# Reordering the prologue of a two-layer graph kernel: first loads, first pairs' nodes and propagators, and the preparation of the output weights

## The chip, the cores and the metric

The kernel runs on one core of a Trainium2 chip. The metric is the device time of one execution in microseconds (us): the median of three runs, beside which one further execution was profiled. In the text PE is the matrix engine, DVE the vector engine, ACT the scalar engine, POOL the GpSimd engine and SP the engine that only issues transfers (DMAs). SPq and ACTq are the DMA-issuing instructions of SP and ACT.

## The reference

There are 128 graphs of 128 nodes with 512 features. Layer 0 is an attention over eight heads, layer 1 a hypergraph convolution with a hidden width of 1024; each is followed by a residual sum and a layer norm.

```python
def _L0_gnn_ref(X, A, W, b, a_self, a_neigh):
    feats = jnp.einsum('bnf,hfu->bhnu', X, W)
    e_self = jnp.einsum('bhnu,hu->bhn', feats, a_self)
    e_neigh = jnp.einsum('bhnu,hu->bhn', feats, a_neigh)
    dense = e_self[..., :, None] + e_neigh[..., None, :]
    dense = jax.nn.leaky_relu(dense, negative_slope=0.2)
    dense = dense + NEG_BIG * (1.0 - A[:, None, :, :])
    att = jax.nn.softmax(dense, axis=-1)
    out = jnp.einsum('bhij,bhju->bhiu', att, feats) + b[None, :, None, :]
    ...
    return jax.nn.relu(out)
...
def hypergraph_conv(x, adj, W, b):
    H = (adj != 0).astype(x.dtype)
    w = adj.reshape(N, -1)[:, :C]
    xw = jnp.einsum('ncd,hd->nch', x, W)
    Dn = jnp.einsum('nce,ne->nc', H, w)
    Dn = jnp.where(Dn > 0, 1.0 / Dn, 0.0)
    Be = H.sum(axis=1)
    Be = jnp.where(Be > 0, 1.0 / Be, 0.0)
    m = Be[:, :, None] * jnp.einsum('nce,nch->neh', H, xw)
    out = Dn[:, :, None] * jnp.einsum('nce,neh->nch', H, m)
    return out + b
...
h = jax.nn.relu(hypergraph_conv(x, adj, W1, b1))
h = layer_norm(h, gamma, beta)
return hypergraph_conv(h, adj, W2, b2) + x
...
x = _layernorm(x + _L0_gnn_ref(x, adj, ...))
x = _layernorm(x + _L1_gnn_ref(x, adj, ...))
```

## The kernel before, in words

Graphs are worked two at a time: 64 pairs, p = 0 to 63. Each pair passes five stages of T = 38.6 units of a hand-written clock ("lag" 0 to 4), so that five pairs are in work at once. Every step of a pair is a small Python function with a due time; lines 912 to 933 put all steps of all pairs in one list, sort it by due time and emit it. Due times set nothing but the order: each engine executes its own instructions in that order, waiting for semaphores, and each DMA queue likewise. For the first two pairs, and for work that is done once, the table `first` (lines 893 to 902) and the list `todo` (lines 877 to 891) give own due times. What is emitted in this way before the first full pair is called the prologue here.

The three large weight products use a scheme with seven products of quarter blocks in place of eight, so that each weight matrix needs sums of its blocks. These sums are made once in the prologue: `prepare_first_sums` (L206, by way of `second_sums`, L188) for the attention weights, `prepare_hidden` (L209, its instruction is L215) for the hidden weights, `prepare_output_block_sums` (L255, L192) for the output weights. The output weights are also scaled by gamma and centred first: `prepare_output` (L220) multiplies them by gamma and beta on PE (the tiles pv, 32 matmuls of L228), `prepare_output_sums` (L233) brings these sums to DRAM and back on all partitions (gw, bw_bc), and `prepare_output_blocks` (L245, L250) applies them.

Steps that matter below, for pair p:

- `load` (L95): the adjacency `a` (two buffers) and its first rows `w` (one buffer), by SP. `load_blocks` (L104) loads node features `xb`, `load_edges` (L113) adjacency columns `ab`, one buffer each.
- `nodes` (L303): DVE makes the node degrees from `a` and `w` and transposes them into the tile `dr` (L318), which has one buffer. `write_nodes` (L321, L323) writes `dr` to DRAM (dd_d), `spread_nodes` (L503, L506) reads it back on all partitions into `dnb`, which also has one buffer.
- `edges`, `scale_edges` (L346, L361): the propagator's two factors hT and hB on DVE. `propagator` (L369, L373, PE) multiplies them into pd, `r_evict` (L379, L381, DVE) multiplies pd by `dnb` into R.
- `spread_rows` (L467 on): DVE transposes the attention terms (L473) and SP writes them to DRAM as rd (L481 for pair 0, L483 else). `neighbours` (L491 on, L500) reads them back on all partitions as nb, 2 x 512 KB. Then POOL masks nb (`masked`, L519), ACT applies the leaky relu (L526), DVE takes the maximum (`largest`, L532) and ACT the exponential (L540).
- `attend` (L599, PE, pav), `attended` (L613, L614, DVE), `add_bias` (L623, POOL), `residual` (L630, DVE), `rstds` (L644 DVE, L646 POOL), `first_shift` (L661, DVE), `first_output` (L667, ACT) end layer 0. `propagate` (L690, PE, pz) and the chain ph (L725, PE) start layer 1, `squares` (L776) and `h_sums` (L399) on POOL follow, then the chain py (L417, PE).

SP issues its DMAs in order and stops at one that has to wait. A DMA whose destination buffer is still to be read waits for the last reader, even when that reader comes later in the sorted list on another engine: the load of `ab` for pair 2 has the due time 105.7 and its reader-to-be-awaited `edges` of pair 1 has 110.4.

In the part ahead of the sorted list, SP loads the four blocks of the attention weights (w_raw, L136), then `a` and `w` of pair 0; ACT issues the attention vectors, the node features and edges of pair 0 and the six small vectors (as_bc, an_bc, xb, ab, b0_bc, b2_bc, b1_sb, gb).

Of the kernel before, what the change touches and what calls it, by code (L numbers as in the profile page):

```python
# [8 lines left out]
F32 = mybir.dt.float32  # L9
AF = mybir.ActivationFunctionType  # L10
ALU = mybir.AluOpType
# [9 lines left out]
def kernel(  # L21
# [45 lines left out]
    nc = tc.nc  # L67
    G, N, F = x.shape
    P = 128
    DH = w1t.shape[1]  # L70
# [5 lines left out]
    QU = HALF // 2  # L76
# [3 lines left out]
    B = 32  # L80
    NB = P // B

    const = ctx.enter_context(tc.tile_pool(name="const", bufs=1))
# [11 lines left out]
    def load(p):  # L95
        s = st[p]
        gs = slice(2 * p, 2 * p + 2)
        s["a"] = work.tile([P, 2, N], F32, tag="a", name=f"a_{p}", bufs=2)
        nc.sync.dma_start(s["a"], adj[gs].rearrange("g n e -> n g e"))
        s["w"] = work.tile([P, 2, N], F32, tag="w", name=f"w_{p}")  # L100
        for g in range(2):
            nc.sync.dma_start(s["w"][:, g, :], adj[2 * p + g, 0, :].partition_broadcast(P))

    def load_blocks(p, queue=None):  # L104
        s = st[p]
        gs = slice(2 * p, 2 * p + 2)

        s["xb"] = work.tile([P, 2 * NB, P], F32, tag="xb", name=f"xb_{p}")
        rows = x[gs].rearrange("g (b n) (f c) -> f n (g b) c", b=NB, f=NB)
        for f in range(NB):  # L110
            (queue or nc.sync).dma_start(s["xb"][f * B:(f + 1) * B], rows[f])

    def load_edges(p, queue=None):  # L113
        s = st[p]

        s["ab"] = work.tile([P, 2 * NB, B], F32, tag="ab", name=f"ab_{p}")
        rows = adj[2 * p:2 * p + 2].rearrange("g (b n) (f e) -> f n (g b) e", b=NB, f=NB)
        for f in range(NB):
            (queue or nc.sync).dma_start(s["ab"][f * B:(f + 1) * B], rows[f])


    def block(dst, ap, i, j, rows, cols):
# [8 lines left out]
    w0_sb = const.tile([P, 7, KF // 2, HH, UW], F32, name="w0_sb")  # L131
    w0_12 = work.tile([P, KF // 2, HH, UW], F32, tag="y2", name="w0_12")
# [6 lines left out]
        )  # L139
        w0_blocks.append((dst, raw.rearrange("p k (h u) -> p k h u", h=HH), j))  # L140

    def everywhere(ap, n, name):
        t = const.tile([P, n], F32, name=name)
        nc.scalar.dma_start(t, ap.partition_broadcast(P))
        return t

    as_bc = everywhere(a_self, F, "as_bc")
    an_bc = everywhere(a_neigh, F, "an_bc")
    load(0)
    load_blocks(0, nc.scalar)  # L150
    load_edges(0, nc.scalar)
    b0_bc = everywhere(b0, F, "b0_bc")
    b2_bc = everywhere(b2, F, "b2_bc")
    bw_bc = const.tile([P, F], F32, name="bw_bc")

    b1_sb = const.tile([P, KH], F32, name="b1_sb")
    gb = const.tile([P, 2, KH], F32, name="gb")
    for t, ap in ((b1_sb, b1), (gb[:, 0, :], gamma), (gb[:, 1, :], beta)):
        nc.scalar.dma_start(t, ap.rearrange("(k p) -> p k", p=P))


    w2_sb = const.tile([P, 7, KH // 2, QU + 1], F32, name="w2_sb")
    w2_12 = work.tile([P, KH // 2, QU], F32, tag="hS", name="w2_12")
    w2_blocks = ((w2_sb[:, 0, :, :QU], 0, 0), (w2_12, 0, 1), (w2_sb[:, 1, :, :QU], 1, 0),
                 (w2_sb[:, 2, :, :QU], 1, 1))
# [15 lines left out]
    for i in range(2):  # L181
        t = const.tile([P, 2, H, UW + 1], F32, name=f"ft{i}")
# [2 lines left out]
    dn = const.tile([P, B], F32, name="dn")  # L185
    nc.gpsimd.memset(dn, 0.0)

    def second_sums(w, b12, some=slice(0, 4)):  # L188

        b11, b21, b22, t4, t1, t2, t3 = (w[i] for i in range(7))  # L190
        for dst, in0, in1 in ((t1, b12, b11), (t2, b22, t1), (t3, b22, b12), (t4, b21, t2))[some]:
            nc.vector.tensor_tensor(dst, in0, in1, op=ALU.subtract)  # L192

    def prepare_first(half):
        for n, (dst, raw, j) in list(enumerate(w0_blocks))[2 * half:2 * half + 2]:
# [8 lines left out]
                nc.vector.tensor_reduce(dst[:, :, :, c], t, AX.X, ALU.add)  # L204

    def prepare_first_sums():  # L206
        second_sums([w0_sb[:, i] for i in range(7)], w0_12)

    def prepare_hidden(i):  # L209
        a11, a12, a22, s1, s2, s3, s4 = (w1_sb[:, i] for i in range(7))  # L210
# [41 lines left out]
                    op0=ALU.mult, op1=ALU.subtract,  # L252
                )

    def prepare_output_block_sums(some):  # L255
        second_sums([w2_sb[:, i, :, :QU] for i in range(7)], w2_12, some)

    def prepare_mean_columns():
        for i in (0, 1, 5):
# [610 lines left out]
    def o_norm(p, s):  # L870
# [5 lines left out]
    T = 38.6  # L876
    todo = [
        (11.1, prepare_first, (0,)), (12.0, prepare_first, (1,)), (77.9, prepare_first_sums, ()),
        (11.8, load_blocks, (1,)), (15.65, load, (1,)), (15.7, load_edges, (1,)),
        (15.8, load_weights, (w2_blocks, w2t, DH // 2, QU)),  # L880
        (16.0, load_weights, (w1_blocks[:2], w1t, F // 2, HALF)),
        (80.2, load_weights, (w1_blocks[2:], w1t, F // 2, HALF)),
        (103.0, prepare_output, ()), (116.5, prepare_output_sums, ()),
        (112.0, prepare_hidden, (0,)), (112.5, prepare_hidden, (1,)),
        (114.5, prepare_hidden, (2,)), (115.0, prepare_hidden, (3,)),
        (122.4, prepare_output_blocks, (slice(0, 2),)),
        (128.4, prepare_output_blocks, (slice(2, 4),)),
        (130.6, prepare_output_block_sums, (slice(0, 2),)),
        (132.8, prepare_output_block_sums, (slice(2, 4),)),
        (100.0, prepare_mean_columns, ()),  # L890
    ]

    first = {
        ("nodes", 0): 15.0, ("write_nodes", 0): 16.5, ("spread_nodes", 0): 18.5,
        ("x_transpose", 0): 11.5, ("edges", 0): 15.2, ("scale_edges", 0): 15.4,
        ("spread_rows", 0): 13.5, ("neighbours", 0): 14.0, ("load_rows", 0): 14.2,
        ("propagator", 0): 103.5, ("r_evict", 0): 104.0,
        ("nodes", 1): 17.6, ("write_nodes", 1): 17.9, ("x_transpose", 1): 14.5,
        ("edges", 1): 110.4, ("scale_edges", 1): 110.5,
        ("spread_rows", 1): 79.9, ("neighbours", 1): 80.0,  # L900
        ("propagator", 1): 117.7, ("r_evict", 1): 118.0,
    }
# [9 lines left out]
    for p in range(PAIRS):  # L912
        if p > 1:
            todo.append((p * T, load, (p,)))
            todo.append((p * T + 19.0, load_blocks, (p,)))
            todo.append((p * T + 28.5, load_edges, (p,)))
        for lag, time, name, since, fn, args in steps:
            if p < since:
                continue
            if p == 0 and lag == 2 and time < 8.5:  # L920
                time *= 0.2
            if p == PAIRS - 1:

                time = {
                    ("attend", 0): 24.25, ("attended", 0): 25.5, ("add_bias", 0): 25.6,
                    ("h_sums", 0): 19.1, ("h_sums", 1): 19.2,
                    ("product", 2): 25.0 if (lag, time) > (3, 20.0) else time,
                }.get((name,) + args[:1], time)
            todo.append((first.get((name, p), (p + lag) * T + time), run, (fn, p, args)))
# [46 lines left out]
```

## Time and profile before

| | |
|---|---|
| median of three runs | 2586.89 us (2586.15 to 2587.33) |
| profiled execution | 2588.48 us; span of the trace 2586.4 us |
| busy: PE, DVE, POOL, ACT | 2515.8, 2146.5, 1714.1, 1514.4 us |
| mean granted PE clock | 0.989 |
| first matmul of L454 (attention features of pair 0) | 19.41 us |
| first matmul of pv (L228) | 65.08 us |
| first matmul of pair 1's second-stage pav (L599) | 117.71 us |

Times within the trace count from the first instruction. "Idle before" and "waits" are time in which an engine stood still, with what ended it. A line such as `DMA dd_d<-dr` names a transfer by destination and source. In a timeline each row is a run of equal instructions: start, duration, engine, line, operation, out<-in, number.

### The profile page before, as it was taken

What the parts mean: (1) busy time and instruction counts of PE and PEld (TensorE: products, weight loads), DVE (VectorE), ACT (ScalarE), POOL (GpSimd) and SP (SyncE); (2) the same over time, 40 slices, a digit from 0 to 9 for tenths busy, and PEclk for the clock granted to TensorE, in tenths of its full rate; (3) what the DMA queues carried; (4) which work ended last, traced back from release to release, by engine and by line L of the source; (5) the groups of instructions that cost most, each with busy time, mean ns of one, the idle gap of its engine ahead of it and who ended that gap; (6) DMA issues with size and microseconds to landing.
All of it is one profiled execution on the core that took longest, in us unless ns stands there. A gap on an engine that the chain in (4) does not pass through costs nothing.

```text
span 2586.4 us, 48239 instructions
## 1 busy us (share of the span) xinstructions
PE 2515.8 (97%) x16312; PEld 2274.8 (88%) x16312; DVE 2146.5 (83%) x4650; ACT 1514.4 (59%) x4293; POOL 1714.1 (66%) x1797
## 2 busy tenths in 40 slices
PE   4799999999999999999999999999999999999997
PEld 3699899899999999989899999999989998999996
DVE  4788888888888888888888888888888888888875
ACT  2365565565565565565565665665665665665662
POOL 1567667667667667667667667667667667667753
PEclk8899999999999999999999999999999999999999
DMA  5444444444444444444444444444444444444430
GB/s 146 116 135 132 143 136 132 143 137 132 142 138 132 142 138 132 145 135 132 135 139 137 137 139 136 136 142 134 135 141 137 134 143 135 134 141 137 135 118 33
DMA packets 428250, 345.57 MB, mean 134 GB/s; under 512 B 146658, under 2 KB 377058, under 8 KB 428004
## 3 DMA queue, kind: packets, MB, share of 16 engines
q1 hardware_dynamic: 422132, 340.77, 44.5%
q10 hardware_dynamic: 5872, 1.72, 0.4%
q8 instruction: 130, 2.13, 0.3%
q14 instruction: 116, 0.95, 0.1%
HBM read 240.66 MB, written 101.72 MB: 132 GB/s over the span
## 4 chain that ended last, share of the span: by engine, by line
PE 89%; DMA 4%; DVE 3%; issue 2%; POOL 2%; SPq 0%; ACT 0%; ACTq 0%; POOLq 0%; DVEq 0%
PE phX L725 17%; PE pyX L417 14%; PE phW L725 9%; PE pfX L417 8%; PE pyW L417 8%; PE pav L599 8%; PE phY L725 4%; PE pz L690 4%; PE pq L849 4%; PE pfW L417 4%; PE pyY L417 4%; PE pfY L417 2%; DMA nb<-rd 1%; PE pd L373 1%; DMA dnb<-dd_d 1%
## 5 line engine op out<-in xcount | busy, mean ns | idle before, releaser
L519 POOL TENSOR_TENSOR nb<-nb,neg 128x512 f32<-128x512 f32 x256 | 320.0, 1272 | 117.9 <-DMA nb<-rd 75.0
L725 PEld LDWEIGHTS phX<-zS,w_sb 128*128 128x128 f32 x3072 | 364.8, 193 | 37.5 <-issue 37.5
L293 ACT COPY py<-pyX 128x257 f32<-128x257 f32 (+1 forms) x192 | 71.7, 374 | 548.0 <-PE pyX L417 548.0
L725 PE MATMUL phX<-zS,w_sb 128*128 128x128 f32 x3072 | 376.0, 276 | 7.1 <-issue 7.1
L776 POOL TENSOR_TENSOR sq<-sq 128x512 f32<-128x512 f32 (+2 forms) x384 | 344.9, 898 | 32.4 <-ACT sq L765 11.3
L526 ACT ACTIVATE nb<-nb,ft 128x128 f32<-128x128 f32 x1024 | 325.2, 389 | 50.1 <-POOL nb L519 48.0
L540 ACT ACTIVATE nb<-nb,nm 128x128 f32<-128x128 f32 x1024 | 320.2, 392 | 17.9 <-DVE nm L532 17.9
L646 POOL TENSOR_TENSOR rso<-veo,mhalf 128x2 f32<-128x2 f32 x64 | 44.8, 700 | 344.3 <-DVE veo L644 302.6
L630 DVE SCALAR_TENSOR_TENSOR y<-y,x 128x512 f32<-128x512 f32 x128 | 155.6, 1216 | 137.9 <-POOL y L623 137.9
L599 PEld LDWEIGHTS pav<-ft,eT 128*128 128x128 f32 x2048 | 251.4, 194 | 11.8 <-issue 2.6
L755 ACT ACTIVATE h<-h,b_sb 128x128 f32<-128x128 f32 x768 | 242.1, 392 | 16.9 <-DVE h L740 16.9
L417 PE MATMUL pyX<-w_sb,hS 128*128 128x257 f32 (+1 forms) x1024 | 248.1, 384 | 2.2 <-DVE hS L399 1.8
L599 PE MATMUL pav<-ft,eT 128*128 128x65 f32 x2048 | 246.5, 274 | 2.5 <-DVE eT L561 1.9
L417 PE MATMUL pyW<-w_sb,hS 128*128 128x256 f32 x1024 | 244.1, 380 | 3.7 <-DVE y L808 3.2
L417 PE MATMUL pyX<-w_sb,h 128*128 128x257 f32 (+1 forms) x1024 | 243.2, 379 | 0.0
L623 POOL TENSOR_TENSOR y<-y,b_bc 128x512 f32<-128x512 f32 x128 | 162.1, 1266 | 95.1 <-DVE y L614 95.1
L417 PEld LDWEIGHTS pyW<-w_sb,hS 128*128 128x128 f32 x1024 | 192.1, 189 | 37.2 <-DVE y L808 10.2
L417 PEld LDWEIGHTS pyX<-w_sb,hS 128*128 128x128 f32 x1024 | 190.2, 191 | 28.0 <-issue 2.1
L417 PEld LDWEIGHTS pyX<-w_sb,h 128*128 128x128 f32 x1024 | 189.3, 190 | 24.9
L399 POOL TENSOR_TENSOR xS<-xT 128x256 f32<-128x256 f32 x124 | 117.9, 951 | 89.5 <-DVE xT L337 89.5
L532 DVE TENSOR_REDUCE nm<-nb 128x4 f32<-128x512 f32 x256 | 173.6, 679 | 0.4 <-ACT nb L526 0.4
L293 ACT COPY ph<-phX 128x512 f32<-128x512 f32 x192 | 112.3, 585 | 97.0 <-PE phX L725 93.8
(127 smaller groups left out, 5843.2 us busy)
## 6 DMA issues: line engine op xcount, KB each, us to landing
nb<-rd SPq DMA_DIRECT2D x128, 512.0 KB, 5.9
ed<-nb SPq DMA_DIRECT2D x126, 512.0 KB, 3.2
eb<-ed SPq DMA_DIRECT2D x504, 128.0 KB, 2.9
x<-in_x_dram SPq DMA_DIRECT2D x64, 512.0 KB, 6.9
out_dram<-o SPq DMA_DIRECT2D x64, 512.0 KB, 2.8
xb<-in_x_dram SPq DMA_DIRECT2D x252, 128.0 KB, 3.0
a<-in_adj_dram SPq DMA_DIRECT2D x64, 128.0 KB, 6.1
w<-in_adj_dram SPq DMA_DIRECT2D x128, 64.0 KB, 3.9
```

The costliest lines, as they stand in the source:

```text
L293: nc.scalar.copy(t[:, :n], s[kind, "X"][:, :n])
L417: nc.tensor.matmul(to[:, :n], lhs[:, k, :], rhs[:, k, :n], start=bool(start) and k == 0, stop=(k == nk - 1), skip_group_check=True,)
L519: nc.gpsimd.tensor_tensor(t, t, neg[:, :, None, :].to_broadcast([P, NB, HH, B]), op=ALU.add)
L526: nc.scalar.activation(t, t, AF.Prelu, bias=s["ft"][:, g, h, 0:1], alpha=SLOPE)
L532: nc.vector.tensor_reduce(s["nm"][:, g, hs], scores(p, s, g, hs).rearrange("p b h j -> p h b j"), AX.XY, ALU.max, negate=True,)
L540: nc.scalar.activation(t, t, AF.Exp, bias=s["nm"][:, g, h:h + 1])
L599: nc.tensor.matmul(t[:, h * (U + 1):(h + 1) * (U + 1)], s["eT"][:, g, q * HH + h, :], s["ft"][:, g, q * HH + h, 2:], start=True, stop=True,)
L623: nc.gpsimd.tensor_tensor(s["y"][:, g, :], s["y"][:, g, :], b0_bc, op=ALU.add)
L630: nc.vector.scalar_tensor_tensor(y, y, 0.0, s["x"][:, g, :], op0=ALU.max, op1=ALU.add)
L725: nc.tensor.matmul(to[:, m * N:(m + 1) * N], w[:, k, m * P:(m + 1) * P], rhs[:, k, :], start=bool(start) and m == 0 and k == 0, stop=(k == ...
L755: nc.scalar.activation(dst[:, k, :], src[:, k, :], AF.Relu, bias=b1_sb[:, c:c + 1])
L776: nc.gpsimd.tensor_tensor(t[:, :n, :], t[:, :n, :], t[:, n:2 * n, :], op=ALU.add)
```

## The change

The due times are those of the sorted list. What changes:

- ACT issues two DMAs only (as_bc, an_bc). The node features, `a` and `w`, and the edges of pair 0 are all issued by SP, in this order, after w_raw. The other vectors become a step `load_vectors`, issued by SP at 15.75: gamma, beta, b1 (L159 before), then b0 and b2 on all partitions.
- `write_nodes` of pair 0 goes from 16.5 to 15.72, which is before the output weights (15.8) and half of the hidden weights (16.0); `spread_nodes` of pair 0 from 18.5 to 15.9, between these two.
- `nodes` of pair 1 goes from 17.6 to 79.95, `write_nodes` of pair 1 from 17.9 to 80.1. The first is now after `spread_rows` of pair 1 (79.9) on DVE, and after `load` of pair 2 (77.2) in the list; the second is after `neighbours` of pair 1 (80.0) and before the second half of the hidden weights (80.2) on SP.
- `propagator` of pair 0 goes from 103.5 to 102.9, ahead of `prepare_output`; `r_evict` of pair 0 from 104.0 to 110.3.
- `prepare_hidden` goes from 112.0 to 115.0 to 110.6 to 111.6, `edges` and `scale_edges` of pair 1 from 110.4 and 110.5 to 112.0 and 112.1, `prepare_output_sums` from 116.5 to 114.2.
- `prepare_output_blocks` goes from 122.4 and 128.4 to 123.2 and 125.2. The first two of the four block sums of the output weights move from DVE to POOL and from 130.6 to 125.6, the other two stay on DVE (132.8 to 133.0).

```diff
+    everywhere(as_bc, a_self, nc.scalar)
+    everywhere(an_bc, a_neigh, nc.scalar)
+    load_blocks(0)
+    load(0)
+    load_edges(0)
+
+    def load_vectors():
+        for t, ap in ((gb[:, 0, :], gamma), (gb[:, 1, :], beta), (b1_sb, b1)):
+            nc.sync.dma_start(t, ap.rearrange("(k p) -> p k", p=P))
+        everywhere(b0_bc, b0, nc.sync)
+        everywhere(b2_bc, b2, nc.sync)
...
-    def second_sums(w, b12, some=slice(0, 4)):
+    def second_sums(engine, w, b12, some=slice(0, 4)):
...
-            nc.vector.tensor_tensor(dst, in0, in1, op=ALU.subtract)
+            engine.tensor_tensor(dst, in0, in1, op=ALU.subtract)
...
-        (15.8, load_weights, (w2_blocks, w2t, DH // 2, QU)),
+        (15.75, load_vectors, ()), (15.8, load_weights, (w2_blocks, w2t, DH // 2, QU)),
...
-        (103.0, prepare_output, ()), (116.5, prepare_output_sums, ()),
-        (112.0, prepare_hidden, (0,)), (112.5, prepare_hidden, (1,)),
-        (114.5, prepare_hidden, (2,)), (115.0, prepare_hidden, (3,)),
-        (122.4, prepare_output_blocks, (slice(0, 2),)),
-        (128.4, prepare_output_blocks, (slice(2, 4),)),
-        (130.6, prepare_output_block_sums, (slice(0, 2),)),
-        (132.8, prepare_output_block_sums, (slice(2, 4),)),
+        (103.0, prepare_output, ()), (114.2, prepare_output_sums, ()),
+        (110.6, prepare_hidden, (0,)), (110.7, prepare_hidden, (1,)),
+        (111.5, prepare_hidden, (2,)), (111.6, prepare_hidden, (3,)),
+        (123.2, prepare_output_blocks, (slice(0, 2),)),
+        (125.2, prepare_output_blocks, (slice(2, 4),)),
+        (125.6, prepare_output_block_sums, (nc.gpsimd, slice(0, 2))),
+        (133.0, prepare_output_block_sums, (nc.vector, slice(2, 4))),
...
-        ("nodes", 0): 15.0, ("write_nodes", 0): 16.5, ("spread_nodes", 0): 18.5,
+        ("nodes", 0): 15.0, ("write_nodes", 0): 15.72, ("spread_nodes", 0): 15.9,
...
-        ("propagator", 0): 103.5, ("r_evict", 0): 104.0,
-        ("nodes", 1): 17.6, ("write_nodes", 1): 17.9, ("x_transpose", 1): 14.5,
-        ("edges", 1): 110.4, ("scale_edges", 1): 110.5,
+        ("propagator", 0): 102.9, ("r_evict", 0): 110.3,
+        ("nodes", 1): 79.95, ("write_nodes", 1): 80.1, ("x_transpose", 1): 14.5,
+        ("edges", 1): 112.0, ("scale_edges", 1): 112.1,
```

More of the change, by code (lines that the diff above doesn't have):

```diff
@@ L102, in load, with load_blocks @@
             nc.sync.dma_start(s["w"][:, g, :], adj[2 * p + g, 0, :].partition_broadcast(P))
-    def load_blocks(p, queue=None):
+    def load_blocks(p):
         s = st[p]
@@ L110, in load_blocks, with load_edges @@
         for f in range(NB):
-            (queue or nc.sync).dma_start(s["xb"][f * B:(f + 1) * B], rows[f])
-    def load_edges(p, queue=None):
+            nc.sync.dma_start(s["xb"][f * B:(f + 1) * B], rows[f])
+    def load_edges(p):
         s = st[p]
@@ L118, in load_edges @@
         for f in range(NB):
-            (queue or nc.sync).dma_start(s["ab"][f * B:(f + 1) * B], rows[f])
+            nc.sync.dma_start(s["ab"][f * B:(f + 1) * B], rows[f])
     def block(dst, ap, i, j, rows, cols):
@@ L140, with everywhere @@
         w0_blocks.append((dst, raw.rearrange("p k (h u) -> p k h u", h=HH), j))
[L142 to L154, printed above, removed]
+    def everywhere(t, ap, queue):
+        queue.dma_start(t, ap.partition_broadcast(P))
+    as_bc, an_bc, b0_bc, b2_bc, bw_bc = (
+        const.tile([P, F], F32, name=n) for n in ("as_bc", "an_bc", "b0_bc", "b2_bc", "bw_bc")
+    )
     b1_sb = const.tile([P, KH], F32, name="b1_sb")
     gb = const.tile([P, 2, KH], F32, name="gb")
-    for t, ap in ((b1_sb, b1), (gb[:, 0, :], gamma), (gb[:, 1, :], beta)):
-        nc.scalar.dma_start(t, ap.rearrange("(k p) -> p k", p=P))
+    everywhere(as_bc, a_self, nc.scalar)
[8 more added lines that the diff above has]
+        everywhere(b2_bc, b2, nc.sync)
     w2_sb = const.tile([P, 7, KH // 2, QU + 1], F32, name="w2_sb")
@@ L206, in prepare_first_sums @@
     def prepare_first_sums():
-        second_sums([w0_sb[:, i] for i in range(7)], w0_12)
+        second_sums(nc.vector, [w0_sb[:, i] for i in range(7)], w0_12)
     def prepare_hidden(i):
@@ L253, in prepare_output_blocks, with prepare_output_block_sums @@
                 )
-    def prepare_output_block_sums(some):
-        second_sums([w2_sb[:, i, :, :QU] for i in range(7)], w2_12, some)
+    def prepare_output_block_sums(engine, some):
+        second_sums(engine, [w2_sb[:, i, :, :QU] for i in range(7)], w2_12, some)
     def prepare_mean_columns():
```

## The prediction, made before the change was run

> **What bounds the kernel now.** I read the page first, then the chain of waits, then the waits and timelines of the first 140 us.
>
> ```profile
> PE 2515.8 (97%) x16312; PEld 2274.8 (88%) x16312; DVE 2146.5 (83%) x4650; ACT 1514.4 (59%) x4293; POOL 1714.1 (66%) x1797
> ...
> PE 89%; DMA 4%; DVE 3%; issue 2%; POOL 2%; SPq 0%; ACT 0%; ACTq 0%; POOLq 0%; DVEq 0%
> ```
>
> PE is the bound, and from 117.71 us the chain is PE alone, one stage of about 38.8 us after another (pyW at 134.40, pz at 136.28, the next pz at 175.09). The change touches nothing there. So it is worth what it moves the start of this row: everything ahead of 117.71 us, of which PE idles half. These waits of the first 125 us tell where:
>
> ```profile
> ACT nb L540 <- DVE nm L532: 17.9, 2, 10.9
> ...
> DVE dr L318 <- DMA dd_d<-dr: 9.0, 1, 9.0
> DVE R L381 <- PE pd L373: 8.1, 1, 8.1
> ```
>
> The middle one is the key. The DVE sits in `nodes` of pair 1 because `dr` has one buffer and the write of pair 0's `dr` stands in SP's queue behind the weights; `largest`, next on DVE, comes late, and ACT's exponentials idle 10.9 us. SP's timeline shows the write and its neighbours:
>
> ```profile
> 43.31 0.68 SPq L123 DMA_DIRECT2D w<-in_w1t_dram  x1
> 44.04 9.21 SPq L323 DMA_DIRECT2D dd_d<-dr  x2
> ...
> 54.33 1.23 SPq L102 DMA_DIRECT2D w<-in_adj_dram  x2
> 60.28 0.33 SPq L483 DMA_DIRECT2D rd<-rows  x1
> 61.86 1.56 SPq L500 DMA_DIRECT2D nb<-rd  x2
> 63.46 1.57 SPq L123 DMA_DIRECT2D w_sb<-in_w1t_dram  x2
> ```
>
> The chain has "44.04 8.53 DMA dd_d<-dr": landed at 52.57.
>
> **What the Trainium skill says.** "DMA: Bandwidth & Descriptors", section "Queues, rings and completion order": each DMA engine takes descriptors in ring order, and SP has one ring on each. The trace agrees: 16 KB took 8.53 us behind 3 MB of weights. The same page, "Rules for kernel authors": a last dimension that isn't contiguous becomes one descriptor per element; b1, gamma and beta are such loads, each 4 KB with 3.7 us to landing. "SBUF — State Buffer", "Who interferes with whom": a DVE instruction with two SBUF inputs contends with a GpSimd one that reads SBUF. The trace agrees: POOL's sum of 128x512 (L399) takes 1.27 us alone, two took 3.48 beside DVE's L192, one of which took 2.18 against 1.22. "TensorE: Matmul & The Clock Gate", Part 1: after idling PE runs at half clock until it has been busy some us. Here the clock is 0.50 from 46 to 69 us; eight pv matmuls take 3.58 us then, sixteen 3.62 later.
>
> **The change, step by step.**
>
> *Front.* ACT issues DMAs until 17.41, loads its table at 17.44, and only then copies the weights:
>
> ```profile
> 14.68 2.04 DVE L337 STREAM_TRANSPOSE xT<-xb 128x512 f32<-128x512 f32 x2 [2.27 <-DMA xb<-in_x_dram]
> ...
> 18.73 1.14 ACT L196 COPY w_sb<-w_raw 128x512 f32<-128x512 f32 x2
> ...
> 19.41 3.89 PE L454 MATMUL pf<-w_sb,xT 128*128 128x264 f32 x8 [19.41 <-ACT w_sb L196]
> ```
>
> Without these issues ACT is done with its copies by about 12.5. PE then waits for xT. xb no longer has `a` and `w` (256 KB, some 1.5 us at 170 GB/s, between the 108 and 279 of that stretch) ahead of it: it lands near 13.0, not 14.6, and xT is ready at 15.2. PE starts there: 4.2 us earlier (bounds: 2.7, if xb lands as before; 4.5). Everything up to nb of pair 0 moves with it: nb issued at 29.3, not 33.44.
>
> *Wait at `nodes` of pair 1 removed.* DVE takes `largest` when ACT is ready: exponentials begin 4.2 + 10.9 = 15.1 us earlier, and pair 1's rows are transposed at 60.02 - 15.1 = 44.9 instead of 60.02. This is the most the front can give.
>
> *The wait comes back at `nodes` of pair 2.* On DVE, `nodes` 1 (79.95) and `nodes` 2 (88.2) now both stand between `spread_rows` 1 and `attended` 0 (99.7), on which gbs, pv and all that follows hang. `nodes` 2 writes `dr` and must wait for `write_nodes` 1, which SP has behind `load` 2 (its `w` waits for `nodes` 1), rd and 1 MB of nb. First, rd has to get through the ring. From nb's first landing (33.44 + 3.95 = 37.39) to dd_d's at 52.57, the ring carried 4.5 MB in 15.2 us, 295 GB/s. Now it carries before rd also b0 and b2 (512 KB, 1.8 us at that rate), the three element-wise vectors (unseen on SP; 0.2 us each like dd_d after the weights, up to 0.9; I take 0.5, so 1.5), dnb, `a` and `w` (384 KB, 1.3) and rd itself (0.2). 37.39 - 4.2 + 15.2 + 4.8 = 53.2. nb follows at 53.4. Both halves landed 9.0 us after the first issue at 61.86 (8.6 + 0.42, the longer of the two) with w1 behind them, 7.5 us (median first landing 5.9, the second about 1.5 later) in the steady part; I take 8.2. dd_d 0.2 after: 61.8. Then the transpose (0.3), `attended` 0 (76.34 to 77.52: 1.2), gbs (0.3) and PE's start (0.2): pv at 64.0 against 65.08. **So of 15.1 us, 1.1 are left** (bounds 0.0 and 2.0 by nb, -1.5 by the front).
>
> *Propagator 0 ahead of pv, r_evict 0 later.* pd leaves the line after pv (75.30 to 75.80, 0.5) and DVE's R (76.00 to 76.34) no longer stands before `attended` 1: **0.6**. R's 0.4 comes back on DVE later, counted there. pv itself stays 9.3 us: PE, idle from about 48, is as cold as before.
>
> *DVE's busy stretch.* From first_shift's end (83.8) to pair 1's eT (116.95) DVE is busy 33.15 us almost without gap. Going out: two block sums,
>
> ```profile
> 110.48 1.22 DVE L192 TENSOR_TENSOR w_sb<-w,w_sb 128x1024 f32<-128x1024 f32 x1
> 111.72 2.18 DVE L192 TENSOR_TENSOR w_sb<-w_sb 128x1024 f32<-128x1024 f32 x1
> ```
>
> 3.4 us; coming in: R, 0.4. Against it stand three things. (1) gw: sums 0.7, then sums_d 1.2 and gw 3.63; before, 5 us of other DVE work filled this. Now sums_d is in SP's queue behind pair 2's `ab`, which waits for `edges` 1, now later, and behind 512 KB of pair 1's x (3.9 to landing): gw lands about 16.9 us after first_shift, DVE is ready at 15.6 to 17.5: 0 to 1.3 lost. (2) `edges` 1 after the hidden sums: PE's pd of pair 1 and with it ph start 4.5 us later, so h_sum waits 0 to 1.9; this overlaps with (1). (3) POOL's two sums of 128x1024 take 2 x 2.5 = 5.0 us (twice its 1.27 for 128x512), with DVE's two-input work beside them up to 7.5, and DVE's fourth sum reads the second: eT then comes at 31.8 to 34.4 after first_shift, against 33.15. PE's own 7.1 us wait at ph (98.7 to 105.84) goes, since pair 1's last `largest` is now before the gw work, but DVE would still decide. I take **0.2** gain (bounds -1.3, +1.4).
>
> Priced at nothing: SP's five more issues (about 0.45 each; SP waits for landings there anyway) and the weights' later landing (pv reads them after 64 us).
>
> **Sum**: 1.1 + 0.6 + 0.2 = 1.9 us. 2586.4 - 1.9 = 2584.5 for the trace's own span; the runs' median is 0.5 above that span, so **2585.0**.
>
> **Rivals.** (a) *The second wait is short*: if `write_nodes` 1 lands before DVE needs it, `nodes` 2 still needs its `w`, which the ring delivers at about 53; `attended` 0 ends at 56.2, pv starts at 56.6: 8.5 + 0.8 = 9.3 gained, 2577.6. For it: dd_d of pair 3, issued at 109.86, took 2.9 us. Against: the ring order that made it 8.53 here. (b) *POOL becomes the bound (slower)*. Place: POOL between x_sums and `squares` of pair 0. Idle there from 101.5 to 111.5 before, it now runs the two sums from about 26 us after first_shift. With full contention (7.5 us) `squares` start 33.2 after first_shift, not 27.7, and `add_bias` of pair 1 ends 5.5 later; ACT's y had 1.4 us of slack against pz (134.86, 136.28), so pz slips by 4.1: 1.1 + 0.6 - 4.1 is 2.4 lost, 2589.3. It decides once `add_bias` 1 ends more than 3.1 us later, counted from first_shift. Against: 0.6 to 2.3 is likelier. (c) *The ring is slower still*: pair 2's dd_d landed at 75.4, 13.5 us after nb; the same for pair 1 gives pv at 69.3: 4.2 - 0.8 = 3.4 lost, 2590.3. Against: that one stood behind 1 MB of w1 as well; here it stands before.
>
> **How the numbers follow.** Chances: forecast 0.50 (own range 2582 to 2588.5), (a) 0.25, (b) 0.13, (c) 0.12. A measurement here can tell about 0.2% (5.2 us) from no change, so faster is below 2581.7 and slower above 2592.1. Faster: 0.25 of (a) and 0.07 of the forecast's edge. Slower: 0.15, the halves of (b) and (c) with both mechanisms or larger sizes. The rest, 0.53, is within. Half of (a) and the slow tail lie outside 2576.5 to 2591.5.
>
> **What would show it.** Right: first L454 matmul near 15.2; DVE without its 9 us at 43 us; two new DVE waits after `nodes` of pair 1, first for pair 2's `w` until about 53, then some 7 us at L318, ended by dd_d; pv at 63 to 65. Wrong: L318 waits under 3 us, pv before 60, rd landing before 50, or PE waiting for POOL's hS or for y around 125 to 140.

## The result, and the profile after

The changed kernel takes **2592.6 us** (median of six runs, 2591.7 to 2599.6) against 2586.5 us (2585.1 to 2588.0) for the kernel before: ratio 1.0029, 95% interval 1.0016 to 1.0042. It is slower by 6.1 us, where 1.9 us of gain were forecast, and lies above the forecast's range, which ended at 2591.5. Line numbers of the changed kernel are two higher than before from `prepare_first` on (L318 is now L320, L740 is L742).

The page comes first: busy times of the engines, and shares of the chain that ended last.

```profile
PE 2510.0 (97%) x16312; PEld 2271.5 (88%) x16312; DVE 2146.1 (83%) x4648; ACT 1514.6 (58%) x4293; POOL 1719.6 (66%) x1799
...
PE 89%; DMA 5%; DVE 3%; issue 1%; POOL 1%; SPq 0%; ACT 0%; POOLq 0%; DVEq 0%; ACTq 0%
```

PE is still the bound, and hardly anyone has more work: POOL has two instructions and 5.5 us more, DVE two fewer. So the loss is again in where PE's unbroken row begins. The clean yardstick is the first pz matmul of each pair, from PE's timeline (start, duration, engine, line, operation, out<-in, number, idle before). Of the kernel before:

```profile
84.71 3.79 PE L690 MATMUL pz<-R,y 128*128 128x128 f32 x16 [7.91 <-ACT y L667]
136.12 1.95 PE L690 MATMUL pz<-R,y 128*128 128x128 f32 x16
```

and of the changed one:

```profile
85.47 3.78 PE L692 MATMUL pz<-R,y 128*128 128x128 f32 x16 [7.87 <-ACT y L669]
143.70 1.95 PE L692 MATMUL pz<-R,y 128*128 128x128 f32 x16
```

Pair 0 reaches pz 0.76 us later, which is within the scatter of single traces: over all runs below it is at 81.3 to 84.7 us in the five traces with the old front, and at 82.5 to 85.5 in the six with the new one (e6 to e8 left aside). **From pair 0 to pair 1, 51.41 us have become 58.23: 6.8 us lost in one stretch.** From there every pair takes about 38.7 us in both kernels. The two profiled executions differ by 4.4 us in span (2586.4 and 2590.8), not by 7.6, because the long row after pair 1 took 3.2 us less in the second: single pairs of 39 to 40 us lie scattered in it, only in part in the same places. Hence the distance between these two pz, which has little such scatter (51.41 to 51.49 in the five traces in which what lies behind pair 0's pz is as before), is used below beside the medians.

The first matmul came when forecast. The answer to the front's lines of before:

```profile
13.88 2.06 DVE L339 STREAM_TRANSPOSE xT<-xb 128x512 f32<-128x512 f32 x2 [1.13 <-DMA ab<-in_adj_dram]
...
15.11 3.86 PE L456 MATMUL pf<-w_sb,xT 128*128 128x264 f32 x8 [15.11 <-DVE xT L339]
```

15.11, where 15.2 was worked out; how far that is luck is told further down. Then the waits of the first 140 us (engine, line, waited for: us in total, times, longest):

```profile
DVE w L311 <- DMA w<-in_adj_dram: 9.7, 1, 9.7
DVE dr L320 <- DMA dd_d<-dr: 9.4, 1, 9.4
...
PE phW L727 <- DVE h L742: 8.4, 1, 8.4
```

The first two are the wait of `nodes`, moved from pair 1 to pair 2 as predicted. The third is new and was not predicted. SP's and DVE's timelines around the moved wait:

```profile
48.72 1.22 SPq L485 DMA_DIRECT2D rd<-rows  x1
55.17 0.93 SPq L502 DMA_DIRECT2D nb<-rd  x2
56.20 0.45 SPq L325 DMA_DIRECT2D dd_d<-dr  x1
```

```profile
54.82 0.29 DVE L311 SCALAR_TENSOR_TENSOR w<-a,w 128x128 f32<-128x128 f32 x1 [9.68 <-DMA w<-in_adj_dram]
...
65.29 0.21 DVE L320 STREAM_TRANSPOSE dr<-dn 128x32 f32<-128x32 f32 x1 [9.35 <-DMA dd_d<-dr]
```

SP could issue nb only at 55.17, when rd had landed (53.2 in the prediction). Both halves had landed at 65.0, 9.8 us later (8.2), and dd_d at 65.2 (61.8). PE's first pv matmul follows at 66.78, and 17.97 us of idle time stand in front of it.

The stretch that lost the time, on DVE:

```profile
106.78 5.16 DVE L252 SCALAR_TENSOR_TENSOR w_sb<-w_sb,gb,gw 128x256 f32<-128x256 f32 x8
...
112.47 2.56 DVE L366 TENSOR_SCALAR hB<-hT,deg 128x128 f32<-128x128 f32 x2
...
116.22 0.64 DVE L742 TENSOR_TENSOR h<-ph,phW 128x512 f32<-128x512 f32 x1
120.74 0.69 DVE L742 TENSOR_TENSOR h<-ph,phW 128x512 f32<-128x512 f32 x1 [3.87 <-PE phW L727]
```

on POOL:

```profile
106.34 2.56 POOL L194 TENSOR_TENSOR w_sb<-w,w_sb 128x1024 f32<-128x1024 f32 x1 [3.13 <-DVE w L252]
112.09 2.66 POOL L194 TENSOR_TENSOR w_sb<-w_sb 128x1024 f32<-128x1024 f32 x1 [3.20 <-DVE w_sb L252]
```

and on PE:

```profile
106.49 2.02 PE L727 MATMUL phX<-zS,w_sb 128*128 128x128 f32 x16 [0.72 <-issue]
116.92 3.78 PE L727 MATMUL phW<-zT,w_sb 128*128 128x128 f32 x16 [8.41 <-DVE h L742]
```

In the kernel before, the same instructions were on DVE:

```profile
105.09 0.47 DVE L364 TENSOR_SCALAR hB<-hT,deg 128x128 f32<-128x128 f32 x2
...
107.31 3.25 DVE L250 SCALAR_TENSOR_TENSOR w_sb<-w_sb,gb,gw 128x256 f32<-128x256 f32 x8
```

The eight gw instructions thus took 3.25 us and take 5.16 beside POOL's first sum; hB took 0.47 and takes 2.56 beside POOL's second. `h_sum` at 116.22 reads the bank phW, and PE stands still for 8.41 us until it has, before its next product into phW. When that starts, PE's clock has fallen (0.50 from 112 to 118 us): sixteen matmuls take 3.78 us, not 2.57, and DVE waits 3.87 us for them in turn.

### The profile page after: what moved, and what is told of

Its sections match the earlier page's. It is cut to its first block, busy times and chain, and to the rows that moved or that the text cites. A ratio compares the mean times of both kernels' runs of the same rounds, so it can differ in the third digit from the quotient of the medians.

```text
span 2590.8 us, 48244 instructions
## 1 busy us (share of the span) xinstructions
PE 2510.0 (97%) x16312; PEld 2271.5 (88%) x16312; DVE 2146.1 (83%) x4648; ACT 1514.6 (58%) x4293; POOL 1719.6 (66%) x1799
## 4 chain that ended last, share of the span: by engine, by line
PE 89%; DMA 5%; DVE 3%; issue 1%; POOL 1%; SPq 0%; ACT 0%; POOLq 0%; DVEq 0%; ACTq 0%
PE phX L727 18%; PE pyX L419 14%; PE phW L727 9%; PE pfX L419 9%; PE pyW L419 8%; PE pav L601 8%; PE phY L727 4%; PE pz L692 4%; PE pfW L419 4%; PE pq L851 4%; PE pyY L419 3%; PE pfY L419 2%; DMA nb<-rd 2%; DMA rd<-rows 1%; PE pd L375 1%
## 5 line engine op out<-in xcount | busy, mean ns | idle before, releaser
L521 POOL TENSOR_TENSOR nb<-nb,neg 128x512 f32<-128x512 f32 x256 | 321.4, 1277 | 110.6 <-DMA nb<-rd 68.7
L528 ACT ACTIVATE nb<-nb,ft 128x128 f32<-128x128 f32 x1024 | 325.1, 389 | 65.1 <-POOL nb L521 63.2
```

The source lines that it names most:

```text
L521: nc.gpsimd.tensor_tensor(t, t, neg[:, :, None, :].to_broadcast([P, NB, HH, B]), op=ALU.add)
L528: nc.scalar.activation(t, t, AF.Prelu, bias=s["ft"][:, g, h, 0:1], alpha=SLOPE)
```

## The experiments

Four theories were set against one another; the expectations use these letters. **O**: `h_sum` of pair 1's second block (L742 at 116.22) now stands behind both halves of the block weights, and PE's wait for it is the loss. **P**: POOL's two sums slow DVE beside them, and this is the loss. **F**: the front, the moved wait included, is the loss. **W**: dd_d landing behind nb is all that keeps pv at 66 us; if `dr`'s write goes ahead of nb or `nodes` 2 goes late, the front's gain of 10 us and more appears. "Stretch" is the distance from pair 0's first pz matmul to pair 1's.

### e1: that h_sum early

```diff
+            early = {("copy", 0, 11.0): 125.12, ("h_sum", 0, 11.8): 125.15}
+            due = first.get((name, p), (p + lag) * T + time)
-            todo.append((first.get((name, p), (p + lag) * T + time), run, (fn, p, args)))
+            todo.append((early.get((name, p, time), due), run, (fn, p, args)))
```

> Changed kernel, with one thing moved: ACT's third copy of ph and DVE's h_sum(1,1) of pair 0 come ahead of the second half of prepare_output_blocks (due times 125.12 and 125.15). Theory O (order): PE's fourth-block product into the bank phW may start only when h_sum(1,1) has read that bank; it stood behind both halves of prepare_output_blocks, so PE waited 8.4 us and DVE then 3.9 us for PE. Then PE's wait at phW falls below 1 us, DVE's 3.9 us go, pair 1's eT comes near 120.4 instead of 124.4, and the time falls by 3 to 5 us to about 2589. Theory P (POOL): the loss is DVE slowed by POOL's two block sums, and PE's wait only follows from it; eT stays within 1.5 us of 124.4, time 2591 to 2593. Theory F (front): the loss is made before first_shift; no change, 2592.6.

Measured: 2591.2 us against 2583.7, ratio 1.0029 (1.0017 to 1.0040). The stretch is 58.12, 0.1 us less. On DVE theory O came true: pair 1's eT begins 36.26 us after the end of `first_shift`, not 39.82, where P had it within 1.5 us of the changed kernel's. But this does not reach pz. PE's timeline:

```profile
105.52 1.95 PE L727 MATMUL phW<-zT,w_sb 128*128 128x128 f32 x16
...
117.42 2.10 PE L419 MATMUL pfX<-w_sb,xS 128*128 128x264 f32 x4 [6.38 <-ACT pf L295]
119.31 3.52 PE L601 MATMUL pav<-ft,eT 128*128 128x65 f32 x16
```

The wait at phW is gone, and PE waits a few products later instead, 6.38 us for ACT's copy of pf, which stands on ACT behind work that waits for the other `h_sum`. Now this idle time stands right ahead of PE's row, and the row begins at a clock of 0.51 (118 to 126 us): sixteen pav matmuls take 3.52 us, where they take 1.90 in the changed kernel. So the wait at phW does cost DVE its part (3.6 us), but to take it away alone gains nothing; theory O falls in so far as it had the time fall by 3 to 5 us.

### e2: the two sums back on DVE, at their old time

```diff
-        (125.6, prepare_output_block_sums, (nc.gpsimd, slice(0, 2))),
+        (130.6, prepare_output_block_sums, (nc.vector, slice(0, 2))),
```

> Changed kernel, with the first two block sums of the output weights back on DVE at their old due time 130.6. Theory O: h_sum(1,1) is reached about 4 us earlier since POOL no longer slows DVE (second half of the blocks 3.2 us instead of 5.2, scale_edges 0.5 instead of 2.6), PE's wait at phW falls from 8.4 to about 4.4, DVE has 2.5 to 3.4 us more to do; time falls by 3 to 5 us, to about 2588.5. Theory P: all of the loss goes, 2586 to 2587. Theory F: no gain, or a loss of 2 to 3 us from the work put back on DVE.

Measured: 2588.2 us against 2583.7, ratio 1.0015 (1.0008 to 1.0021); stretch 53.92, 4.3 us less. DVE's timeline shows what returned:

```profile
104.79 3.24 DVE L252 SCALAR_TENSOR_TENSOR w_sb<-w_sb,gb,gw 128x256 f32<-128x256 f32 x8
...
108.56 0.47 DVE L366 TENSOR_SCALAR hB<-hT,deg 128x128 f32<-128x128 f32 x2
```

5.16 is 3.24 again and 2.56 is 0.47: 4.0 us, with 2.45 us of sums taken back on DVE, and PE's wait at phW shrinks from 8.41 to 3.96; eT begins 35.81 us after `first_shift`. POOL's sums are the greater part of the loss in the stretch, 4.3 of 6.8 us. The medians show less of it: each beside its own runs of the kernel before, e2 is still 4.5 us slower, the changed kernel 6.1. P had all of the loss going; O's figures for this run (a wait of 4.4 us, 2588.5 us) were nearer.

### e3: both

The edits of e1 and e2 together.

> Changed kernel with both: h_sum(1,1) ahead of the second half of the blocks, and the two block sums on DVE. Theory O and P together (each a part): no wait of PE at phW, no slow DVE instructions from 106 to 115 us, eT near 118.7, time about 2587, within 1.5 us of the kernel before. Theory F: 2592 or more.

Measured: 2592.0 us against 2583.7, ratio 1.0033 (1.0020 to 1.0045); stretch 57.60. The two remedies together are worse than the second alone by 3.7 us, though DVE reaches eT 35.1 us after `first_shift`'s end, against 35.8 in e2. PE's timeline tells why:

```profile
117.08 2.10 PE L419 MATMUL pfX<-w_sb,xS 128*128 128x264 f32 x4 [5.20 <-ACT pf L295]
118.97 3.51 PE L601 MATMUL pav<-ft,eT 128*128 128x65 f32 x16
```

and so do busy time and granted clock in windows (start:end, length, busy us of PE, PEld, DVE, ACT, POOL, then PE's clock, DMA share, GB/s). Of e3:

```profile
112.00:118.00 6.00, 0.93 (x2) 0.84 (x3) 5.93 (x8) 2.07 (x6) 1.25 (x1) 0.87 0.57 152
118.00:126.00 8.00, 8.00 (x28) 6.88 (x27) 3.90 (x10) 1.29 (x3) 7.14 (x7) 0.50 0.01 3
```

and of e2:

```profile
112.00:118.00 6.00, 6.00 (x31) 5.44 (x31) 4.86 (x5) 4.81 (x14) 3.39 (x3) 0.85 0.72 171
118.00:126.00 8.00, 7.63 (x50) 6.70 (x48) 6.01 (x14) 1.67 (x4) 7.84 (x7) 1.00 0.02 3
```

In e3 PE has done its matmuls early, then idles, and begins the row at clock 0.50: 28 matmuls in 8 us, where e2 does 50 at full clock. In e2 the product at phW comes late, and by the time pav begins the clock is up. The idle time just ahead of the row is paid twice here, first as idling and then in slow matmuls; the earlier one is hidden.

### e4: the kernel before with the change of blocks and sums alone

```diff
-        (122.4, prepare_output_blocks, (slice(0, 2),)),
-        (128.4, prepare_output_blocks, (slice(2, 4),)),
-        (130.6, prepare_output_block_sums, (slice(0, 2),)),
-        (132.8, prepare_output_block_sums, (slice(2, 4),)),
+        (123.2, prepare_output_blocks, (slice(0, 2),)),
+        (125.2, prepare_output_blocks, (slice(2, 4),)),
+        (125.6, prepare_output_block_sums, (nc.gpsimd, slice(0, 2))),
+        (133.0, prepare_output_block_sums, (nc.vector, slice(2, 4))),
```

> Kernel before, with only the change of the output blocks: prepare_output_blocks at 123.2 and 125.2, the first two block sums on POOL at 125.6, the other two at 133.0. Theories O and P: PE again waits at phW for h_sum(1,1), 6 to 9 us, with first_shift ending at 83.8 as before; eT 5 to 7 us later than 116.95; time 2591 to 2593, so nearly the whole loss. Theory F: no loss, 2585 to 2587.

Measured: 2590.0 us against 2583.7, ratio 1.0023 (1.0015 to 1.0030); stretch 56.92, 5.5 more than before. In the old prologue these four lines alone give most of the loss; the 1.3 us from 56.92 to 58.23 belong to the rest of the change, which no run takes apart. Its DVE shows the same two rows as the full change, to the hundredth:

```profile
102.45 5.16 DVE L250 SCALAR_TENSOR_TENSOR w_sb<-w_sb,gb,gw 128x256 f32<-128x256 f32 x8
...
108.14 2.56 DVE L364 TENSOR_SCALAR hB<-hT,deg 128x128 f32<-128x128 f32 x2
```

### e9 and e10: its two halves

e9 is the kernel before with the block weights at 123.2 and 125.2 and all four sums left on DVE at their time; e10 leaves the block weights and puts the first two sums on POOL.

```diff
# e9
-        (122.4, prepare_output_blocks, (slice(0, 2),)),
-        (128.4, prepare_output_blocks, (slice(2, 4),)),
+        (123.2, prepare_output_blocks, (slice(0, 2),)),
+        (125.2, prepare_output_blocks, (slice(2, 4),)),
# e10
-        (130.6, prepare_output_block_sums, (slice(0, 2),)),
+        (130.6, prepare_output_block_sums, (nc.gpsimd, slice(0, 2))),
```

> Kernel before, with prepare_output_blocks at 123.2 and 125.2 only; all block sums stay on DVE at 130.6 and 132.8. If the order of the blocks is what costs (h_sum(1,1) behind both halves): PE waits 8 us or more at phW and the time rises by 4 to 6 us, as with the whole change of the output blocks. If POOL is what costs: DVE passes the second half in 3.2 us, PE waits 3 to 5 us at phW, eT stays within 1 us of before (33.2 us after first_shift), and the time rises by 0 to 2 us.

> Kernel before, with the first two block sums of the output weights on POOL, at their old place 130.6. If POOL beside DVE is what costs at any place: DVE's instructions beside the two sums are slowed as in the changed kernel and the time rises by 3 to 6 us. If it costs only together with the new order: here h_sum(1,1) and the second half of the blocks are already done when POOL starts, PE has no wait at phW, and the time rises by 0 to 3 us, by POOL's later squares and add_bias.

Measured: e9 2585.3 us against 2584.6, ratio 1.0005 (0.9997 to 1.0014), stretch 52.04; e10 2586.8, ratio 1.0008 (1.0002 to 1.0015), stretch 53.83. Apart they add 0.6 and 2.4 us to the 51.4 of before, together (e4) 5.5. In e9 PE waits 7.19 us at phW, in place of the 7.10 at phX before, and is yet in time, since DVE's row is hardly longer than it was (eT 33.93 us after `first_shift`, before 33.14); in e10 the second sum on POOL runs after the gw work (109.78 to 112.14) and slows the sums that DVE kept:

```profile
110.17 3.06 DVE L192 TENSOR_TENSOR w_sb<-w_sb,w 128x1024 f32<-128x1024 f32 x1
113.15 2.28 DVE L192 TENSOR_TENSOR w_sb<-w_sb 128x1024 f32<-128x1024 f32 x1
```

These are 5.34 us, where the same two took 2.68 in the kernel before; its first sum on POOL (100.94) stands beside two of DVE's `output` instructions (L678), 2.88 us for 1.28. That is 4.26 us more, against the 3.40 of sums that DVE gave up: eT begins 34.02 us after `first_shift`, PE waits 2.28 us for it and then has a clock of 0.79 (118 to 126 us), so that the stretch grows by more than eT's delay. With the blocks early as well, POOL's sums run beside the gw work and hB and ahead of `h_sum`, so their delay falls on DVE *and* on PE's wait for DVE, and PE then starts cold. That product of the two edits is what neither has alone. (The two runs do not split e4 exactly: e10's first sum stands at 130.6, e4's at 125.6.)

### e5: the changed kernel with only the front left

Back to their old time go the propagator and r_evict of pair 0, `edges` and `scale_edges` of pair 1, the hidden weights, the output sums, the blocks, and the block sums (back on DVE too).

```diff
-        (103.0, prepare_output, ()), (114.2, prepare_output_sums, ()),
-        (110.6, prepare_hidden, (0,)), (110.7, prepare_hidden, (1,)),
-        (111.5, prepare_hidden, (2,)), (111.6, prepare_hidden, (3,)),
+        (103.0, prepare_output, ()), (116.5, prepare_output_sums, ()),
+        (112.0, prepare_hidden, (0,)), (112.5, prepare_hidden, (1,)),
+        (114.5, prepare_hidden, (2,)), (115.0, prepare_hidden, (3,)),
...
-        ("propagator", 0): 102.9, ("r_evict", 0): 110.3,
+        ("propagator", 0): 103.5, ("r_evict", 0): 104.0,
...
-        ("edges", 1): 112.0, ("scale_edges", 1): 112.1,
+        ("edges", 1): 110.4, ("scale_edges", 1): 110.5,
```

> Changed kernel with everything from propagator 0 onwards put back (propagator, r_evict, edges, hidden sums, output sums, output blocks and block sums as in the kernel before): only the loads, the vectors and nodes/write_nodes/spread_nodes of pairs 0 and 1 are changed. Theory W (the wait only moves): DVE waits about 9 us for pair 2's w and 9 us more for dd_d, pv starts near 66.8, the stretch behind it is that of before; the time is within 2 us of the kernel before. Theory F (the front is what costs): 3 us or more slower.

Measured: 2588.0 us against 2583.9, ratio 1.0016 (1.0009 to 1.0022). The stretch is 51.49, that of before, so the whole 6.8 us of the stretch are in what e5 takes back. By the medians it is otherwise: they are 4.1 us up, as F had it (3 us or more) and W had not (within 2 us), and pair 1's pz in the trace gives no reason for it (134.15, before 136.12). One profile of each on one chip followed, to see where the 4 us are:

> The kernel before, unchanged, profiled beside the others on the same chip: the distance from the first pz of pair 0 to the first of pair 1 is 51.4 us as before; the first pz of pair 0 at 82.5 to 85, the spread of the first transfers.

> The kernel with the front alone changed, profiled a second time. Theory W (the wait only moves): the first pz of pair 0 within 1.5 us of that of the kernel before on the same chip. If the front costs the 4 us that the rounds showed: 3 to 5 us later, by a later landing of rd, nb or dd_d of pair 1.

before_again: 2584.2 us, pz at 83.60 and 135.08. e5_again: 2588.4 us, pz at 84.29 and 135.77. So 0.7 us lie in the front, all of it between pv (64.23 and 64.18) and pz, and the stretch is 51.48 in both. The other 3.4 us of the 4.1 between the spans lie after pair 1's pz, as scattered pairs of 39 to 40 us. Whether that part belongs to the front is not settled. PE waits longer there for DVE's y (L810, L808 in the kernel before), 4.8 us against 2.7; but from pair 1's pz to the end the fourteen traces of this case take 2446.6 to 2450.7 us, and traces of either front cover most of that. Nor do the medians add up: the four lines of e4 cost 6.4 us with the old front, the front alone 4.1, both in the changed kernel 6.1. So the loss in the stretch is what the runs explain; why the front costs the median 4 us by itself stays open.

### e6, e7, e8: take the moved wait away

e6 is the changed kernel with `write_nodes` of pair 1 ahead of nb on SP (behind the write of rd); e7 also holds `nodes` and `write_nodes` of pair 2 back until DVE is done with gbs and the first statistics of pair 0; e8 is e7's order on e5.

```diff
# e6
-        ("nodes", 1): 79.95, ("write_nodes", 1): 80.1, ("x_transpose", 1): 14.5,
+        ("nodes", 1): 79.95, ("write_nodes", 1): 79.97, ("x_transpose", 1): 14.5,
# e7, and e8 on e5
+        ("nodes", 2): 103.5, ("write_nodes", 2): 103.6,
```

> Changed kernel, with write_nodes of pair 1 at 79.97, ahead of neighbours of pair 1 on SP. Theory W: dd_d no longer stands behind 1 MB of nb and lands with rd near 55; the wait at the second dr transpose (9.4 us) falls below 1 us, the wait for w stays; pv starts near 57.5 instead of 66.8 and the time falls by 8 to 10 us against the changed kernel, to 1 to 4 us under the kernel before. Rival: the time ahead of first_shift is not what sets the end (DVE or the transfers of nb and the hidden weights catch up with it); under 4 us of fall.

> As the one before, and nodes and write_nodes of pair 2 at 103.5 and 103.6, behind the first residual: attended 0 and gbs wait for nothing of pair 2. Theory W: no wait of DVE for w or dd_d ahead of pv; pv starts at 49 to 51, when the output weights have landed, first_shift ends 15 us earlier than in the changed kernel, and the time falls by 13 to 16 us against it, about 8 us under the kernel before. Rival: pv or the masks then wait for the weights or for nb in the same ring, and half of it or less is seen.

> The same order of nodes and write_nodes, on the kernel with the front alone changed (propagator, edges, hidden sums, output blocks and their sums as in the kernel before). Theory W with the loss in the output blocks: about 6 us faster than with the changed output blocks, 13 to 16 us under the kernel before. Rival: the stretch behind first_shift becomes longer when it starts earlier, since the hidden weights' second half and nb land at 65 to 68; 8 us or less under the kernel before.

| kernel | wait at L311 | wait at L320 | pv | stretch | median, before | ratio |
|---|---|---|---|---|---|---|
| changed | 9.68 | 9.35 | 66.78 | 58.23 | 2592.6, 2586.5 | 1.0029 (1.0016 to 1.0042) |
| e6 | 9.07 | 0.03 | 54.46 | 58.22 | 2582.5, 2583.9 | 0.9995 (0.9987 to 1.0003) |
| e7 | 2.81 | 0.04 | 47.23 | 61.20 | 2576.2, 2583.9 | 0.9969 (0.9957 to 0.9980) |
| e8 | 3.82 | 0.04 | 45.87 | 51.44 | 2571.9, 2583.9 | **0.9951 (0.9938 to 0.9963)** |

Theory W holds for pv: one line of SP's order moves it by 12 us (by 9 to 10 against the other traces of the same front, 63.5 to 64.2), two more by another 7. For the time it holds less well: e6's gain over the kernel before is within the noise, and e8, for which 13 to 16 us were expected, has 12.0. The DVE of e6 shows `dr` free as soon as it is reached, and SP's own row why (dd_d at 46.98, nb at 52.22):

```profile
46.98 0.51 SPq L325 DMA_DIRECT2D dd_d<-dr  x1
52.22 0.92 SPq L502 DMA_DIRECT2D nb<-rd  x2
```

e7 keeps the second half of the change, and pays 61.2 us for its stretch (why 3 us more than in the changed kernel, no run takes apart). e8 keeps the front and leaves the second half out: it beats both kernels, by **12 us** against the kernel before. In e8 PE reaches pv with almost no wait (0.89 us) and pair 1's pz at 116.85, 18 to 19 us ahead of the two traces of the kernel before (135.08, 136.12). Why only 12 of these are in the median is as open as the 4 us of e5:

```profile
116.85 1.95 PE L692 MATMUL pz<-R,y 128*128 128x128 f32 x16
```

## Why the prediction was wrong, step by step

**Front**: right in kind, PE waits for xT; that the number fits is luck. The last piece of xb landed at 13.80, not near 13.0, and PE started after the first of xT's two transposes, 1.3 us later, where both were counted (2.2): two errors that cancel. (The profile puts xT's own wait down to ab, which xT does not read and which landed at 14.6 to 15.1.) In the eight other traces with this front the first matmul comes at 12.3 to 12.9, in the four others with the old one at 17.5 to 18.4: a gain of about 5 to 6 us, where 4.5 was the upper bound.

**Wait at `nodes` of pair 1 removed, and it comes back at `nodes` of pair 2**: the mechanism was right, shown by both waits in the profile and by e6, in which dd_d goes ahead of nb and the second one is 0.03 us. Pair 1's rows are transposed at 43.67 (44.9 worked out). In this trace the sum was mis-sized by 2.8 us, in three terms. rd landed at 55.04, not 53.2 (+1.8). nb took 9.8 us from issue to its second landing, not 8.2 (+1.6). dd_d landed 0.2 after nb, as assumed. These 3.4 became 2.8 at pv (66.78, not 64.0), since what lies between dd_d's landing and pv took 1.6 us, where the prediction has 2.2 (its own terms give 2.0). So instead of 1.1 us gained at pv, 1.7 were lost against the 65.08 of before, a place between the forecast and rival (c), the slower ring. Much of this is scatter: in the five other traces with this order pv comes at 63.5 to 64.2, and in the five with the old order at 62.1 to 65.1. What is certain is that of the front's 15 us hardly anything is left at pv.

**Propagator 0 ahead of pv, r_evict 0 later**: 0.6 was taken. From pv to the end of `first_shift` it went from 18.73 us (65.08 to 83.81) to 17.79 (66.78 to 84.57), 0.9 less; some of it is pv itself, 9.3 to 8.8. Right in kind.

**DVE's busy stretch**: this is the step that failed. A gain of 0.2 was taken (bounds -1.3 and +1.4), and 6.7 us were lost: from `first_shift`'s end to pair 1's eT, 33.14 us became 39.82. Point by point:

- (1), gw: it was to land 16.9 us after `first_shift`, with DVE ready at 15.6 to 17.5. It landed at 18.0 (102.58), DVE was ready at 17.8, and the gw work began 18.04 us after `first_shift`, against 14.90 before: **3.1 us later**, of which only 0.2 is waiting for gw. The rest is DVE's own row: R 0.4, as counted; three short waits 1.0 with that one (0.29 at `h_sum`, 0.48 at a `largest`, 0.23); one `largest` 0.6 that came after the gw work's first half before; hB 0.7 less (1.42 to 0.70); and the hidden weights' sums, 2.03 and 2.18 us where they took 1.21 and 1.23, 1.8 more (e5, with them at their old place, has 1.21 and 1.22). Before, these started at 87.21, after POOL's row of `nb` additions and masks (82.53 to 86.61); now they start at 84.83 beside that row (L521, 83.29 to 87.99). Moving them forward was priced at nothing.
- (3), POOL's sums: their own price was right, 2.56 and 2.66 against 2.5 each. **What was left out is the price for DVE beside them**: the gw work +1.9 and hB +2.1. The contention was charged to POOL alone (5.0 to 7.5 us), although the prediction's own lines show a DVE sum (L192) of 2.18 us for 1.22, beside POOL's `squares` (L776) and not beside the L399 that it names. The Trainium skill ("SBUF — State Buffer", "Who interferes with whom") says that a DVE instruction with two SBUF inputs contends with a GpSimd one that reads SBUF, that `tensor_scalar` can enter a mode which takes the shared port pair as well, and that in such a mode the engine which issues first has the pair for its whole instruction and the other is blocked. The trace agrees instruction by instruction: the first gw instruction beside POOL's sum took 2.39 us and ended at 109.18, just after POOL's at 108.90, and the other seven took 0.47 each; the first hB took 2.36 and ended at 114.83, just after POOL's at 114.75, the second 0.27. e2 gives 0.47 for both hB without POOL's sum.
- (2), the hidden sums ahead of `edges`, was said to let `h_sum` wait 0 to 1.9 us. It waits 3.87, and not because ph started late (5.7 us later, where 4.5 was said): PE could not fill phW, since DVE had not yet read it; the `h_sum` that reads it stands behind both block halves now. **That chain DVE, PE, DVE was in no step**, though the diff shows the second half go from 128.4 to 125.2 past it. And "PE's own 7.1 us wait at ph goes": it did, and one of 8.41 at phW came in its place.

From the gw work on, the sum closes. Before, it took 18.24 us from 98.71 to eT at 116.95, after, 21.78 from 102.61 to 124.39: 3.5 more. Taken out: 3.4 of sums, 1.0 in the first block half (4.73 to 3.73) and 0.6 of one `largest` that now comes earlier. Added: 1.9 and 2.1 of contention, 3.87 of waiting, 0.5 in the sums that stayed (3.21 for 2.68). That is 8.4 - 5.0 = 3.4. With the 3.1 ahead of the gw work it makes the 6.5 of the 6.7.

**From eT to pz** nothing more was lost: 116.95 to 136.12 is 19.17 before, 124.39 to 143.70 is 19.31 after. The rest of the trace's sum is 0.76 at `first_shift`: 0.76 + 6.82 = 7.6 at pair 1's pz, 4.4 in the span, and 6.1 between the medians.

The **rivals**: (b) had POOL as the place and contention as the mechanism, yet put it behind `squares` and `add_bias`, late by 5.5 us, with y's slack of 1.4 as the point of decision. POOL's sums did come out slow for DVE, not late for `squares`: `squares` wait 5.70 us for ACT there. Its 2589.3 was nearer, by another path. (c) had the slower ring, and is borne out in part at pv, and in this one trace. That the result was outside the range comes from the bounds of DVE's busy stretch: they were made of what the moved instructions cost, and not of what waits for each of them in turn.

**What was said would show it wrong** was looked for in the wrong places: L320 waiting under 3 us, pv before 60, PE waiting for hS or y. None came true, and the forecast's own signs came nearly all, one of them by luck (15.11, two waits after `nodes` of pair 1; pv at 66.8 was past the 63 to 65), so the front of the trace read as a confirmation while the loss lay 40 us later.

## What to carry to other kernels

When an instruction is moved to another engine, price its neighbours and not only itself: list what runs at that time on the engine that shares its ports, and add to that engine's row the time for which it may be held (here up to the length of each moved instruction, 2.4 us). When something is moved ahead of an instruction that frees a PSUM bank, follow the bank: which matmul writes it next, and what waits for that. A wait that is removed by reordering can come back at the next user of the same single buffer, as it did here; one write ahead of a large read, and the next user held back, were worth 16 us more than the reordering without them.

## What the runs showed of the hardware that was not expected

- PE's clock makes an idle time cost by its place. The Trainium skill ("TensorE: Matmul & The Clock Gate", Part 1) has half clock after some us of idling; the trace agrees: here the clock was 0.50 from 118 to 126 us in e3, after 5.2 us of idling right ahead of pav, and e3's stretch is 3.7 us longer than that of e2, which has a wait of 3.96 some 6 us earlier and clock 1.00 there. In e9 7.19 us at phW, in place of 7.10 at phX before, cost the stretch only 0.6.
- Contention between DVE and POOL fell on DVE in the gw work: POOL's sums of 128x1024 took 2.56 and 2.66 us, about twice its 1.27 for half the size, while DVE's eight instructions went from 3.25 to 5.16. It fell on one of the eight: the first was held until POOL's sum had ended (2.39 us for 0.47 in the changed kernel and in e4, 1.80 in e1), and the rest ran at their usual time. In e10 POOL ran 2.36 beside DVE's 3.06 and 2.28. In the kernel before, it was POOL whose two sums of 128x512 took 3.48.
- The first transfers land differently from run to run: the first matmul comes at 12.3 to 12.9 us in eight traces with the new front and at 15.1 in that of the changed kernel, and 17.5 to 19.4 in those with the old.
